# Spreading a block's scatters over the next block, and three smaller moves, in a macaron layer on one core

## The chip, the cores and the metric

One Trainium2 chip, one of its cores. The time is the device time in microseconds of one launch of the whole program; a few launches are timed and their median is given. Beside it stands one execution that the hardware profiler recorded; all durations below come from that one.

## The reference, cut to what matters

4096 tokens of width 256 (two sequences of 2048) go through three residual steps: half a feed-forward step, attention, half a feed-forward step again, each on a layer-normed input.

```python
x = x + 0.5 * ffn(layernorm(x))
x = x + attn(layernorm(x))
x = x + 0.5 * ffn(layernorm(x))
...
# ffn
logits = rmsnorm(x) @ router_w.T            # 8 experts, the best 2 of them for each token
dispatch = first 640 tokens of each expert  # in token order
routed   = scatter_add(w * (silu(xg @ rg) * (xg @ ru)) @ rd)   # inner width 1024
shared   = (silu(x @ sg) * (x @ su)) @ sd                      # inner width 2048
return shared + routed
...
# attn: groups of 64 tokens, 16 heads of 16
q, k = rmsnorm(q) * ln_w, rmsnorm(k) * ln_w
y = softmax(causal(q @ k.T / 4)) @ v
return y @ w_proj
```

The two feed-forward steps use the same weights. Float32 results are wanted; the kernel gets them from float16 matmuls by splitting each operand into a high and a low float16 part and summing three products.

## The kernel before

**Names of the work.** A *tile* is 128 tokens, a *block* is 512 tokens or four tiles; there are 32 tiles and 8 blocks. The shared expert's inner width of 2048 is cut into 16 *chunks* of 128. For a chunk and a block, `gate_up` (L339) runs 12 matmuls of 512 columns into two PSUM tiles `pgu` (three buffers; 6 for the gate, 6 for the up projection). ScalarE reads the gate's `pgu` into `sl` (L356 in phase c, L360 elsewhere), VectorE multiplies the gate's `pgu` into it (L357, phase c alone) and then the other `pgu` (L362), ScalarE rounds `sl` to the high part `hh` (L364), VectorE takes the low part `hl` (L365). `down` (L368) then adds 12 matmuls of 256 columns into two PSUM tiles `po`: 8 of them read `hh`, 4 read `hl`. `defer` emits the `down` of a chunk after the `gate_up` of the next one. After the 16th chunk, L406 evicts the two `po` tiles into `xr` on VectorE, and L409 stores them.

**Phases.** Phase a normalises and routes all 32 tiles for the first feed-forward step while it runs shared blocks 0 to 3. Phase b runs the 8 experts of that step. Phase c runs shared blocks 4 to 7 of the first step and blocks 0 to 6 of the second, and beside them attention on all 32 tiles, each followed by the norm and the routing for the second step. Phase d has the experts of the second step and the last shared block.

**What a tile does beside the blocks.** A tile's work is a generator whose steps are *slots*. `drive` (L728) takes one slot for every 3 steps of the shared block in phase c (`RATE_C`), so a block of 48 steps has 16 slots; a new tile starts every `GAP_C` = 4 slots. An attention tile: `stats` (L142) on VectorE and a power on GpSimd (L150, the reciprocal root), `normed` (L152) with a small VectorE instruction for the bias (`nm`, L158) and ScalarE for the result (L160), a DMA transpose, q, k, v matmuls, the squares of q and k on ScalarE (L544), their scaling on VectorE (L545) and a power on GpSimd (L547), q and k scaled on VectorE (L557) and spread on ScalarE (L567, L573) and GpSimd (L568, L574), scores, mask (L590), maximum (L595), exponential, values, projection, and then `stats` and `normed` again for the next step.

**Routing.** When the fourth tile of a block has its logits, `route` (L237) finds the two experts of each token and the row of the expert's list that it gets, and then scatters the tile rows `X` into the list `xg` in DRAM: for each of four tiles, four GpSimd copies (L328) of token number, weights and expert into the row's tail, and two indirect DMAs on GpSimd's queue (L330). One step of `route` issues one tile's scatters, so the four tiles go in four slots in a row. In phase c each is placed behind the last `anchor`, a GpSimd subtraction of an attention tile; phase a sets no anchor.

**Experts.** `expert_load` (L416) loads the 640 list tails of an expert (`tag`, L420) and the 640 rows, transposed (`xe`, L422), and turns the tails into row numbers and weights with four small VectorE instructions (L429 to L433). They are needed at the expert's last chunk, when its output is scattered.

**Order.** The program is emitted in the order above, and a scheduler then lays the instructions out on each engine; `issue_after` puts an instruction behind a given one on its engine, and `behind` does so for the last `gate_up` instructions on ScalarE (0) or VectorE (1). Each engine runs its own queue strictly in order; SyncE's queue issues the plain and transposing DMAs, GpSimd's the indirect ones.

Of the kernel before, what the change touches and what calls it, by code (L numbers as in the profile page):

```python
# [8 lines left out]
F32 = mybir.dt.float32  # L9
# [28 lines left out]
class Net:  # L38
# [103 lines left out]
    def stats(self, x, mv, rstd):  # L142
        nc = self.nc
        st = self.sm.tile([P, 6], F32, name="st")
        nc.vector.bn_stats(out=st, in_=x)
        nc.vector.bn_aggr(out=mv, in_=st)
        ve = self.sm.tile([P, 1], F32, name="ve")
        nc.vector.tensor_scalar(
            out=ve, in0=mv[:, 1:2], scalar1=LN_EPS, scalar2=1.0 / UP ** 2, op0=ALU.add, op1=ALU.mult)
        nc.gpsimd.tensor_tensor(out=rstd, in0=ve, in1=self.mhalf[:, :1], op=ALU.pow)  # L150

    def normed(self, x, mv, rstd, pool=False):  # L152
# [3 lines left out]
        if pool:  # L156
            nm = self.sm.tile([P, 1], F32, name="nm")
            nc.vector.scalar_tensor_tensor(  # L158
                out=nm, in0=mv[:, 0:1], scalar=-1.0, in1=rstd, op0=ALU.mult, op1=ALU.mult)
            nc.scalar.activation(z, x, AF.Identity, bias=nm, scale=rstd)  # L160
# [75 lines left out]

    def route(self, R, b, fb):  # L237

# [60 lines left out]
        if b == NB - 1:  # L299
            self.limits(R)  # L300
            yield
        for t in range(4):
            with self.tc.issue_after(self.anchor.ins) if self.anchor else nullcontext():
                self.scatter(R, b, fb, t, di, w1, dl, ef)
            yield

# [32 lines left out]
    def gate_up(self, wc, x, h, tanh=False):  # L339
# [24 lines left out]
        nc.scalar.copy(h[0], s)  # L364
        nc.vector.tensor_tensor(out=h[1], in0=s, in1=h[0], op=ALU.subtract)  # L365
        yield
# [25 lines left out]
    def shared(self, b, xb, src, dst, tanh=False, late=2):  # L392
        nc = self.nc
        outs = [self.ps_out.tile([P, BT], F32, name="po", tag="po") for _ in range(2)]
        for c in range(16):
# [5 lines left out]
            def fin(c=c, h=h):  # L401
# [3 lines left out]
                for i in range(2):  # L405
                    nc.vector.scalar_tensor_tensor(  # L406
                        out=res[i], in0=outs[i].rearrange("p (t f) -> p t f", f=H), scalar=0.5 / WS,
                        in1=res[i], op0=ALU.mult, op1=ALU.add)
                    nc.sync.dma_start(  # L409
# [6 lines left out]
    def expert_load(self, R, e, hold):  # L416
# [11 lines left out]
        tk = self.sm.tile([P, 5], I32, name="tkb")  # L428
        nc.vector.tensor_tensor(out=tk, in0=tag[:, :, 0].bitcast(I32), in1=R["bits"][:, e], op=ALU.bitwise_and)  # L429
        nc.vector.tensor_tensor(out=ids, in0=tk.bitcast(F32), in1=R["off"][:, e], op=ALU.add)  # L430
        nc.vector.scalar_tensor_tensor(
            out=w, in0=tag[:, :, 3], scalar=float(e), in1=tag[:, :, 1], op0=ALU.is_equal, op1=ALU.mult)
        nc.vector.tensor_tensor(out=w, in0=w, in1=tag[:, :, 2], op=ALU.add)  # L433

# [84 lines left out]
    def attn_tile(self, R, j, x2, new_fb):  # L519
# [23 lines left out]
        for i in range(2):  # L543
            nc.scalar.activation(qk[:, i, :], pqk[:, i, :], AF.Square, scale=1.0 / XP, accum_out=ss[:, i:i + 1])  # L544
        nc.vector.tensor_scalar(  # L545
            out=ss, in0=ss, scalar1=XP ** 2 / H, scalar2=1e-6 * XP ** 2, op0=ALU.mult, op1=ALU.add)
        nc.gpsimd.tensor_tensor(out=ss, in0=ss, in1=self.mhalf[:, :2], op=ALU.pow)  # L547
        pv = self.m1([P, H], F32, "pv")
# [136 lines left out]
class Tiles:  # L685


    def __init__(self, make, count, gap, held=None):
        self.make, self.count, self.gap = make, count, gap
        self.held = held  # L690
        self.slot = 0
        self.live = []
        self.nxt = 0

    def done(self):
        return self.nxt == self.count and not self.live

    def steps(self):

        if self.slot == self.nxt * self.gap and self.nxt < self.count:  # L700
            self.live.append((self.nxt, self.make(self.nxt)))
            self.nxt += 1
        for one in list(self.live):
# [4 lines left out]
            elif r == "stall":  # L708
                return
            yield  # L710
        self.slot += 1
# [36 lines left out]
def macaron(ctx, tc, x, w_qkv, ln_w, w_proj, router_w, rg, ru, rd, sg, su, sd, out):  # L748
# [21 lines left out]
    def tail(R, h, b, t):  # L770
        if t == 3:
            yield from n.route(R, b, fbs[(h, b)])

# [64 lines left out]
RATE_C = 3.0  # L838
GAP_C = 4
XTB = 2  # L840
# [31 lines left out]
```

## Time and profile before

| | us |
|---|---|
| median of 3 runs (lowest, highest) | 1819.73 (1818.86, 1820.77) |
| the profiled execution | 1819.79 |
| its span, first to last instruction | 1817.6 |
| TensorE busy | 1778.5 (98%) |
| VectorE busy | 1190.9 (66%) |
| ScalarE busy | 949.4 (52%) |
| GpSimd busy | 753.4 (41%) |
| scatters L330, 128 of them | 132.3 busy, 27.7 idle on "issue" in between |

The profiled execution lies within the spread of the timed runs, and 2.2 us lie outside its span. How to read it: TensorE is busy for nearly the whole span, so the sum of the other engines' work says little; what matters is where TensorE stands idle and which instruction ends that idle time. In a timeline row, the bracket gives the idle time of the engine just before the instruction and what ended it. A matmul's record is longer than the distance between two starts in a row (records overlap in the pipeline), so an idle bracket of TensorE is somewhat shorter than the time lost there.

### The profile page before, as it was taken

How to read it: one execution, taken by the hardware profiler on the slowest of the kernel's cores; microseconds unless marked ns; L12 is line 12 of the kernel's file. 1: busy time of each engine (PE TensorE's matmuls, PEld its weight loads, DVE VectorE, ACT ScalarE, POOL GpSimd, SP SyncE). 2: the span in 40 equal slices, each digit the busy share in tenths (PEclk: the TensorE clock that was granted, in tenths of full speed). 3: DMA queues.
4: the chain of work that ended last, by engine and by line, in shares of the span. 5: the costliest groups of instructions: out<-in, count | busy, mean ns of one | idle time of the engine just before them, and what ended most of it. 6: DMA issues, size and time to landing. Idle time of an engine off the chain costs nothing. (4 is left out here: it accounts for less than half of the span.)

```text
span 1817.6 us, 37398 instructions
## 1 busy us (share of the span) xinstructions
PE 1778.5 (98%) x13652; PEld 1199.6 (66%) x13652; DVE 1190.9 (66%) x2907; ACT 949.4 (52%) x2055; POOL 753.4 (41%) x1072
## 2 busy tenths in 40 slices
PE   8999999999999899999999999999999999999998
PEld 5665657777777556665656666566655677777765
DVE  7756546666665577877787777777756566666643
ACT  4433334555555466666666666666323455555542
POOL 6576620221111434576767677776430011122210
PEclk9999999999999999999999999999999999999999
DMA  7333133554443455767667676756212144555420
GB/s 216 91 102 112 41 66 84 123 118 111 114 108 71 98 91 101 129 112 141 122 134 135 117 152 111 145 98 127 61 28 66 35 108 109 116 121 118 103 44 12
DMA packets 439193, 185.95 MB, mean 102 GB/s; under 512 B 302305, under 2 KB 436125, under 8 KB 439008
## 3 DMA queue, kind: packets, MB, share of 16 engines
q1 hardware_dynamic: 420528, 161.60, 40.6%
q0 software_dynamic: 17664, 21.17, 6.7%
q8 instruction: 107, 1.75, 0.4%
q10 hardware_dynamic: 816, 0.79, 0.1%
q14 instruction: 78, 0.64, 0.1%
HBM read 78.95 MB, written 42.21 MB: 67 GB/s over the span
## 5 line engine op out<-in xcount | busy, mean ns | idle before, releaser
L349 PE MATMUL pgu<-xb,sgu 128*128 128x512 f16 x3072 | 736.6, 379 | 11.3 <-DVE sl L357 6.9
L364 ACT CAST hh<-sl 128x512 f16<-128x512 f32 (+2 forms) x512 | 272.9, 533 | 529.8 <-DVE sl L362 528.6
L349 PE MATMUL pgu<-xe,wc 128*128 128x384 f16 (+1 forms) x3072 | 497.1, 299 | 0.0
L349 PEld LDWEIGHTS <-sgu 128*128 128x128 f16 x3072 | 292.8, 98 | 284.7 <-issue 16.9
L362 DVE SCALAR_TENSOR_TENSOR sl<-pgu,sl 128x512 f32<-128x512 f32 (+2 forms) x512 | 301.0, 588 | 223.5 <-PE pgu L349 198.1
L365 DVE TENSOR_TENSOR hl<-sl,hh 128x512 f16<-128x512 f32 (+2 forms) x512 | 312.6, 611 | 149.3 <-ACT hh L364 147.9
L373 PEld LDWEIGHTS <-hh 128*128 128x128 f16 x3328 | 321.2, 98 | 109.8 <-ACT hh L364 6.6
L349 PEld LDWEIGHTS <-wc 128*128 128x128 f16 x3072 | 300.6, 98 | 92.0
L373 PE MATMUL po<-sdw,hh 128*128 128x256 f16 x2048 | 350.2, 273 | 5.3 <-ACT hh L364 3.2
L373 PE MATMUL po<-sdw,hl 128*128 128x256 f16 x1024 | 249.8, 273 | 14.0 <-DVE hl L365 11.4
L373 PE MATMUL po<-wd,hh 128*128 128x256 f16 x1280 | 223.6, 273 | 0.0
L472 POOL DMA_INDIRECT out_dram<-eo,eidscatter x40 | 65.2, 1630 | 341.3 <-DVE eo L471 331.6
L373 PEld LDWEIGHTS <-hl 128*128 128x128 f16 x1664 | 162.7, 98 | 56.3 <-DVE hl L365 22.6
L360 ACT ACTIVATE sl<-pgu 128x384 f32<-128x384 f32 (+1 forms) x336 | 159.0, 474 | 60.6 <-PE pgu L349 34.4
L472 POOL DMA_INDIRECT acc<-eo,eidscatter x40 | 65.7, 1642 | 290.3 <-DVE eo L471 280.6
L357 DVE SCALAR_TENSOR_TENSOR sl<-sl,pgu 128x512 f32<-128x512 f32 x176 | 120.2, 683 | 56.1 <-ACT sl L356 54.9
L330 POOL DMA_INDIRECT xg<-X,di x128 | 132.3, 1033 | 49.9 <-issue 27.7
L373 PE MATMUL po<-wd,hl 128*128 128x256 f16 x640 | 152.5, 273 | 0.0
L356 ACT ACTIVATE sl<-pgu 128x512 f32<-128x512 f32 x176 | 104.3, 593 | 39.1 <-PE pgu L349 37.5
L105 ACT ACTIVATE wc<-re 128x512 f16<-128x512 f32 x128 | 80.5, 629 | 74.4 <-PE pgu L349 58.2
L106 DVE SCALAR_TENSOR_TENSOR wc<-re,wc 128x512 f16<-128x512 f32 x128 | 88.3, 690 | 27.6 <-ACT wc L105 27.4
L596 POOL TENSOR_TENSOR S<-S,amx 128x1024 f32<-128x1024 f32 x32 | 63.9, 1997 | 77.9 <-DVE amx L595 70.9
(155 smaller groups left out, 1725.7 us busy)
## 6 DMA issues: line engine op xcount, KB each, us to landing
re<-in_L_ffn_rg_dram SPq DMA_DIRECT2D x128, 128.0 KB, 2.3
re<-in_L_ffn_ru_dram SPq DMA_DIRECT2D x128, 128.0 KB, 2.4
re<-in_L_ffn_rd_dram SPq DMA_DIRECT2D x128, 128.0 KB, 2.3
y<-acc SPq DMA_DIRECT2D x64, 128.0 KB, 2.4
y<-in_L_attn_x_dram SPq DMA_DIRECT2D x32, 128.0 KB, 2.2
acc<-xr SPq DMA_DIRECT2D x16, 256.0 KB, 2.5
out_dram<-xr SPq DMA_DIRECT2D x16, 256.0 KB, 2.7
x<-y SPq DMA_DIRECT2D x28, 128.0 KB, 1.9
```

Of the source, the lines that this page charges most:

```text
L105: nc.scalar.mul(hi, src, WS)
L106: nc.vector.scalar_tensor_tensor(out=lo, in0=src, scalar=WS, in1=hi, op0=ALU.mult, op1=ALU.subtract)
L330: i = nc.gpsimd.indirect_dma_start(out=R["xg"][:, :], out_offset=bass.IndirectOffsetOnAxis(ap=di[:, t, k:k + 1], axis=0), in_=X, in_offset ...
L349: nc.tensor.matmul(p, lhsT=wc[:, w, i, k, :], rhs=x[:, 2 * a + k, :], start=(j == 0), stop=(j == 5))
L356: nc.scalar.activation(s, p, AF.Tanh, scale=0.5 / XP)
L357: nc.vector.scalar_tensor_tensor(out=s, in0=s, scalar=1.0, in1=p, op0=ALU.add, op1=ALU.mult)
L360: self.latest[0] = nc.scalar.activation(s, p, AF.Silu, scale=1.0 / XP).ins
L362: self.latest[1] = nc.vector.scalar_tensor_tensor(out=s, in0=ps[1], scalar=1.0 / XP / (2.0 * XP if tanh else 1.0), in1=s, op0=ALU.mult, op ...
L364: nc.scalar.copy(h[0], s)
L365: nc.vector.tensor_tensor(out=h[1], in0=s, in1=h[0], op=ALU.subtract)
L373: nc.tensor.matmul(o, lhsT=h[a][:, t * P:(t + 1) * P], rhs=wd[:, w], start=(c == 0 and j == 0 and t % 2 == 0), stop=(c == nch - 1 and j == 2),
L472: i = nc.gpsimd.indirect_dma_start(out=R["acc"][:, :], out_offset=bass.IndirectOffsetOnAxis(ap=ids[:, t:t + 1], axis=0), in_=eo, in_offset ...
```

## The change

Four things are done, two of them by giving the scheduler further rules.

1. **Scatters.** `route` no longer runs its four scatter steps itself. They become a generator, `scatters`, handed to `Tiles.extra`; every slot, after the live tiles, takes one step of each such generator. One tile's scatters are issued every `int(gap)` slots: 4 in phase c, 2 in phase a. The last block of each step (`b == NB - 1`) keeps one tile per step. Each tile's scatters go behind the last `anchor`, and `stats` and the power on q's and k's squares now set the anchor too, so there is always one, in phase a as well.
2. **Distance of tiles.** `GAP_C` is 4.25 in place of 4, and a tile starts at the first slot that is not below its number times the gap: slots 0, 5, 9, 13, 17 and so on.
3. **Operands of powers.** GpSimd does the bias `nm` as a product and a multiplication by -1, and the scaling of the squares, in place of VectorE.
4. **Order on VectorE.** The second of the two evictions of a block is placed behind the low part of the chunk just emitted (`self.low`). The four small instructions of `expert_load` are placed behind the last `gate_up` instruction on VectorE.

```diff
 def stats(self, x, mv, rstd):
-        nc.gpsimd.tensor_tensor(out=rstd, in0=ve, in1=self.mhalf[:, :1], op=ALU.pow)
+        self.anchor = nc.gpsimd.tensor_tensor(out=rstd, in0=ve, in1=self.mhalf[:, :1], op=ALU.pow)
 def normed(self, x, mv, rstd, pool=False):
-            nc.vector.scalar_tensor_tensor(
-                out=nm, in0=mv[:, 0:1], scalar=-1.0, in1=rstd, op0=ALU.mult, op1=ALU.mult)
+            nc.gpsimd.tensor_tensor(out=nm, in0=mv[:, 0:1], in1=rstd, op=ALU.mult)
+            nc.gpsimd.tensor_scalar_mul(nm, nm, -1.0)
 def route(self, R, b, fb, tiles):
+        last = self.scatters(R, b, fb, di, w1, dl, ef, 1 if b == NB - 1 else tiles.gap)
+        if b == NB - 1:
+            yield from last
+        else:
+            tiles.extra.append(last)
+
+    def scatters(self, R, b, fb, di, w1, dl, ef, every):
         for t in range(4):
-            with self.tc.issue_after(self.anchor.ins) if self.anchor else nullcontext():
+            with self.tc.issue_after(self.anchor.ins):
                 self.scatter(R, b, fb, t, di, w1, dl, ef)
-            yield
+            for _ in range(int(every)):
+                yield
 def gate_up(self, wc, x, h, tanh=False):
-        nc.vector.tensor_tensor(out=h[1], in0=s, in1=h[0], op=ALU.subtract)
+        self.low = nc.vector.tensor_tensor(out=h[1], in0=s, in1=h[0], op=ALU.subtract).ins
 def shared(...):
                 for i in range(2):
-                    nc.vector.scalar_tensor_tensor(
+                    with self.tc.issue_after(self.low) if i else nullcontext():
+                        nc.vector.scalar_tensor_tensor(
 ...
 def expert_load(self, R, e, hold):
-        nc.vector.tensor_tensor(out=tk, in0=tag[:, :, 0].bitcast(I32), in1=R["bits"][:, e], op=ALU.bitwise_and)
+        with self.behind(True, 1):
+            nc.vector.tensor_tensor(out=tk, in0=tag[:, :, 0].bitcast(I32), in1=R["bits"][:, e], op=ALU.bitwise_and)
 ...
 def attn_tile(self, R, j, x2, new_fb):
-        nc.vector.tensor_scalar(
+        nc.gpsimd.tensor_scalar(
             out=ss, in0=ss, scalar1=XP ** 2 / H, scalar2=1e-6 * XP ** 2, op0=ALU.mult, op1=ALU.add)
-        nc.gpsimd.tensor_tensor(out=ss, in0=ss, in1=self.mhalf[:, :2], op=ALU.pow)
+        self.anchor = nc.gpsimd.tensor_tensor(out=ss, in0=ss, in1=self.mhalf[:, :2], op=ALU.pow)
 class Tiles:
-        if self.slot == self.nxt * self.gap and self.nxt < self.count:
+        if self.slot >= self.nxt * self.gap and self.nxt < self.count:
 ...
+        for g in list(self.extra):
+            if next(g, "end") == "end":
+                self.extra.remove(g)
+            yield
         self.slot += 1
-GAP_C = 4
+GAP_C = 4.25
```

More of the change, by code (lines that the diff above doesn't have):

```diff
@@ L235, in logits, with route @@
         nc.scalar.copy(fb["L"][:, t], p)
-    def route(self, R, b, fb):
+    def route(self, R, b, fb, tiles):
         nc = self.nc
@@ L405, in fin @@
                 for i in range(2):
-                    nc.vector.scalar_tensor_tensor(
-                        out=res[i], in0=outs[i].rearrange("p (t f) -> p t f", f=H), scalar=0.5 / WS,
-                        in1=res[i], op0=ALU.mult, op1=ALU.add)
+                    with self.tc.issue_after(self.low) if i else nullcontext():
+                        nc.vector.scalar_tensor_tensor(
+                            out=res[i], in0=outs[i].rearrange("p (t f) -> p t f", f=H), scalar=0.5 / WS,
+                            in1=res[i], op0=ALU.mult, op1=ALU.add)
                     nc.sync.dma_start(
@@ L428, in expert_load @@
         tk = self.sm.tile([P, 5], I32, name="tkb")
[L429 to L433, printed above, removed]
+        with self.behind(True, 1):
+            nc.vector.tensor_tensor(out=tk, in0=tag[:, :, 0].bitcast(I32), in1=R["bits"][:, e], op=ALU.bitwise_and)
+            nc.vector.tensor_tensor(out=ids, in0=tk.bitcast(F32), in1=R["off"][:, e], op=ALU.add)
+            nc.vector.scalar_tensor_tensor(
+                out=w, in0=tag[:, :, 3], scalar=float(e), in1=tag[:, :, 1], op0=ALU.is_equal, op1=ALU.mult)
+            nc.vector.tensor_tensor(out=w, in0=w, in1=tag[:, :, 2], op=ALU.add)
     def experts(self, R, rg, ru, rd, cur):
@@ L692, in __init__ @@
         self.live = []
+        self.extra = []
         self.nxt = 0
     def done(self):
-        return self.nxt == self.count and not self.live
+        return self.nxt == self.count and not self.live and not self.extra
     def steps(self):
-        if self.slot == self.nxt * self.gap and self.nxt < self.count:
+        if self.slot >= self.nxt * self.gap and self.nxt < self.count:
             self.live.append((self.nxt, self.make(self.nxt)))
@@ L771, in tail @@
         if t == 3:
-            yield from n.route(R, b, fbs[(h, b)])
+            yield from n.route(R, b, fbs[(h, b)], tiles)
     def tile1(j):
```

## The prediction

> **What bounds the kernel now.** I read the page's first part, then busy time by stretch, then looked for every idle bracket of TensorE in the timeline, and last at who holds the instruction that ends it.
>
> ```profile
> PE 1778.5 (98%) x13652; PEld 1199.6 (66%) x13652; DVE 1190.9 (66%) x2907; ACT 949.4 (52%) x2055; POOL 753.4 (41%) x1072
> ```
>
> TensorE is busy for all but 39.1 of 1817.6 us, and the change takes no matmul away. So the most that any reordering can give is these 39 us, about 2%. By stretch (columns: stretch, length, then busy PE, PEld, DVE, ACT, POOL, granted clock, DMA share, GB/s):
>
> ```profile
> 0.00:266.00 266.00, 255.37 (x1698) 154.96 (x1699) 162.49 (x527) 105.11 (x222) 154.60 (x345) 0.99 0.39 107
> 594.00:660.00 66.00, 59.70 (x367) 34.04 (x366) 41.64 (x83) 36.23 (x79) 26.77 (x33) 1.00 0.46 89
> 660.00:1300.00 640.00, 626.22 (x5296) 396.56 (x5295) 492.23 (x1240) 405.27 (x851) 429.48 (x580) 1.00 0.65 121
> 1300.00:1381.00 81.00, 77.40 (x483) 45.51 (x482) 48.79 (x133) 25.66 (x48) 18.23 (x40) 1.00 0.27 59
> ```
>
> Idle: 10.6 us in phase a, 6.3 at the entry of phase c, 13.8 in its steady part, 3.6 at its end; 4.2 are the end of the program. Both expert stretches between have none. In phase a, one place:
>
> ```profile
> 136.33 0.98 POOL L330 DMA_INDIRECT xg<-X,di  x1 [0.30 <-issue]
> 137.45 0.59 POOL L150 TENSOR_TENSOR rstd<-ve,mhalf 128x1 f32<-128x1 f32 x1
> 138.07 0.41 DVE L162 TENSOR_SCALAR z<-y,mv,rstd 128x256 f32<-128x256 f32 x1 [5.08 <-POOL rstd L150]
> 138.49 0.66 DVE L365 TENSOR_TENSOR hl<-sl,hh 128x512 f16<-128x512 f32 x1
> 139.21 0.28 PE L373 MATMUL po<-sdw,hl 128*128 128x256 f16 x1 [2.27 <-DVE ve L148]
> ```
>
> Read upward: TensorE waits for the low part, which stands on VectorE behind L162, which waits for a power on GpSimd, which stands behind eight scatters of 1.28 us each (0.98 and 0.30 of issue). In phase c the same wait for `hl` comes back in every block, with other culprits:
>
> ```profile
> 909.26 0.59 ACT L356 ACTIVATE sl<-pgu 128x512 f32<-128x512 f32 x1
> 909.88 0.69 DVE L357 SCALAR_TENSOR_TENSOR sl<-sl,pgu 128x512 f32<-128x512 f32 x1 [0.55 <-ACT sl L356]
> 910.62 1.46 PE L349 MATMUL pgu<-xb,sgu 128*128 128x512 f16 x6 [0.87 <-DVE sl L357]
> 911.28 0.68 DVE L406 SCALAR_TENSOR_TENSOR xr<-po,xr 128x512 f32<-128x512 f32 x1
> 912.48 0.68 DVE L406 SCALAR_TENSOR_TENSOR xr<-po,xr 128x512 f32<-128x512 f32 x1
> 913.08 0.68 DVE L365 TENSOR_TENSOR hl<-sl,hh 128x512 f16<-128x512 f32 x1
> 913.82 0.28 PE L373 MATMUL po<-sdw,hl 128*128 128x256 f16 x1 [0.71 <-DVE hl L365]
> 934.31 0.28 PE L373 MATMUL po<-sdw,hl 128*128 128x256 f16 x1 [0.74 <-DVE hl L365]
> ```
>
> These three waits (a `pgu` buffer freed late, `hl` behind both evictions and a mask, and 20 us later `hl` behind mask and maximum, L590 and L595) recur every 81.5 us, because 4 slots per tile and 16 per block keep tiles and blocks in step. At the end of phase c small expert instructions, waiting for their DMAs, hold VectorE:
>
> ```profile
> 1378.69 0.17 DVE L429 TENSOR_TENSOR tkb<-tag,scatter1b 128x5 int32<-128x5 int32 x1 [0.60 <-DMA tag<-xg]
> 1379.60 0.68 DVE L406 SCALAR_TENSOR_TENSOR xr<-po,xr 128x512 f32<-128x512 f32 x1
> 1380.34 0.38 PE L373 MATMUL po<-sdw,hh 128*128 128x256 f16 x2 [2.01 <-DVE xr L406]
> ```
>
> **The change part by part.** A bracket is about 0.16 us short of the time lost, since records overlap; I add that to each. Where places are counted I use the order in which the built program puts instructions on each engine, which has no times in it.
>
> *Scatters.* Their number, 128, their four copies each and their DMAs stay. A burst of 8, 10.3 us, becomes four of 2.6 us, each behind a power. Phase a has three stalls at such bursts: 42.86 (1.75 us), 139.21 (2.43), 168.18 (0.54). The one at 139 costs more:
>
> ```profile
> 139.60:143.10 3.50, 3.50 (x14) 1.59 (x12) 3.03 (x19) 1.52 (x3) 0.93 (x5) 0.51 0.51 138
> ```
>
> After 2.27 idle us the granted clock was 0.51 for 3.5 us, so another 1.7 us of matmul time went. The Trainium skill (TensorE: Matmul & The Clock Gate, Part 1) has the clock fall only after at least one idle window of some 3.4 us; by that rule the stall is worth 2.4 us, by the row 4.1. I take the row. With half of the other two (a power may still wait 2.6 us), phase a gives 5.2 of 6.4. What could it cost? Rows `X` stay occupied longer: tile 4 of a block scatters some 19 slots after its norm, its buffer (one of 6) is wanted after 25.5; 6 slots of 5 us are left, so nothing.
>
> *Evictions.* At six boundaries 0.87 us is lost, 5.2 in all. In the new order the first eviction still precedes `hl` at times, the second never, so `hl` comes at least 0.6 us sooner; one boundary has the key and value instructions L552, L557 in front of `hl` instead, and I leave it its loss: 4.4. The added wait: behind the second eviction on VectorE stands the next L357, and on SyncE a store; on TensorE the second half of the new block's `down`, before which the order has 6 gate/up matmuls (1.29 us) against 0.68 of eviction. Zero.
>
> *4.25 slots.* Tiles now drift by one slot per block. I summed, for each chunk of phase c, VectorE's work between L362 and its L365 and set it against the matmul work placed before the first use of `hl`. Before, the stalled chunks are those with 1.9 to 2.0 us in between and 5.1 to 5.3 us of cover, a difference of 3.1 or 3.4; no other chunk in the steady part is below 3.7. In the new order chunks with so much work have 6 us of cover or more, differences of 4.0 and up; two chunks stay below 3.4. So the five stalls of 0.90 behind mask and maximum leave 3.6 of 4.5. The six `pgu` waits of 1.04 (6.2 us) come from ScalarE, where L356 stands behind L567; that happens in three tiles of four now, in one of four then: I take half, 3.1. The last tile starts at slot 132, not 124. In the new order the last routing matmul (L311) stands 33 us of matmul work later but still 48 us ahead of the first expert matmul; from the first of the last scatters (1344.99) to the first split of expert weights (1362.74) the trace has 17.8 us. Nothing is due there.
>
> *Expert instructions.* Moved from the phase's end to some chunk of each expert, with one DMA of tails per expert moved on SyncE past weight loads (their two buffers allow it one expert ahead, some 38 us). The stalls of 1364 to 1380 sum to 4.6. ScalarE's first split stands 12 us behind L311 in the new order against 17.8 needed from nearly there, so part stays: 3.0 gained. Inside experts TensorE has no idle time though more VectorE work (scaling L471 and splits) lies there; four instructions of 0.16 cost zero. If that cover were gone it would be 14 times 0.5 us.
>
> *GpSimd forms operands.* VectorE loses 64 x 0.159 and 32 x 0.169 = 15.6 us and these waits (us in total, times, longest):
>
> ```profile
> DVE nm L158 <- POOL rstd L150: 23.3, 15, 2.8
> DVE nm L158 <- POOL arstd L150: 8.3, 20, 0.7
> ```
>
> GpSimd gains 64 products and 64 scalings; the nearest rows are L244 (0.21) and L245 (0.24 to 0.37), so 0.44 to 0.58 a pair, and 0.24 to 0.37 for the squares: 36 to 49 us over phase c, where it goes from 67% to about 73%. The Trainium skill (GPSIMD Engine Reference, Engine selection) speaks against this: element-wise work belongs on VectorE, GpSimd being about twice as slow on two inputs. The row agrees on the price (0.44 against 0.16), and by the rule alone the sum would be 64 x 0.28 = 18 us of longer chains. But the trace puts the wait between the engines (31.6 us of VectorE standing) above the arithmetic, and these chains have slots to spare. Own value: zero (from -16 as below to +2).
>
> *New waits.* In the new order five places of phase c have ScalarE work between two L356 that exceeds the matmul work by over 1.3 us, against three before. I charge them and a tighter entry of phase c 4.1 us.
>
> Sum: 5.2 + 4.4 + 3.6 + 3.1 + 3.0 - 4.1 = 15.2 us; 1819.79 - 15.2 = 1804.6. The profiled execution is within 0.1 us of the median, so this is also the median that I expect.
>
> **The rivals.** *The stalls move* (0.20). The waits depend on lateness that an order without times doesn't show; half of the 19.3 us goes, the new waits come: 1819.8 - 9.6 + 4.1 = 1814.3. For it: before, three equal stalls per block survived a planned order. Against: the differences of work and cover pick out the stalled chunks.
>
> *GpSimd's longer chain makes it slower* (0.13). The power for q and k now stands behind two subtractions (0.67 each) close in front of it in 14 tiles of 32 and one in 12 (before: 3 and 11), and has one more instruction. If ScalarE's L567, waiting for it, has L356 behind it, `pgu` is freed up to 1.4 us later. With all 15.2 us gained, it decides from 11 tiles on; at 18 tiles, 25 us, the time is 1830. Against: in three tiles of four L356 stands ahead of L567.
>
> *It does not do what it says* (0.07): the spread scatters hold the powers as before, or the late last tile delays the experts, and gains are returned: 1819, slightly slower possible.
>
> **How the numbers follow.** Forecast 0.60, at 1804.6. A measurement of this kernel tells about 0.2% (3.6 us) from no change. Faster: 0.60 and 0.17 of the first rival, 0.77. Same: 0.03 of it and 0.05 of the last, 0.08. Slower: 0.13 and 0.02, 0.15. The range leaves out the slow rival (0.13) above 1819, and below 1796 the case that nearly all of 29 us of stalls goes (0.07).
>
> **What would show it.** Right: no idle bracket over 2 us at the scatters of phase a and no half clock there; no L158 or L545 among VectorE's rows; idle of 660 to 1300 down from 13.8 to 5 or 6; no wait for `tag` on VectorE near the end of phase c. Wrong: brackets of 1 us for L349 behind L357 in most blocks, with L567 waiting for L547's successor on GpSimd; or a new wait for `hl` once per block.

## The result: slower by 0.9%, and the profile after

The changed kernel takes 1834.61 us (median of 6 runs, 1833.94 to 1836.77) against 1819.7 us of the kernel before beside it; the ratio is 1.0087, with a 95% interval of 1.0077 to 1.0097. That is 30 us above the forecast of 1804.6 and outside its range. The profiled execution has a span of 1832.4 us against 1817.6.

The first line is the busy time of the changed kernel's page. In it `gate_up`'s VectorE instructions are L366 and L371, the high part is L373, the low part L374, `down` is L382.

```profile
PE 1781.5 (97%) x13652; PEld 1198.9 (65%) x13652; DVE 1202.6 (66%) x2811; ACT 949.5 (52%) x2055; POOL 802.5 (44%) x1232
```

VectorE has 96 instructions fewer, which were 15.6 us in the profile before, and is busy 11.7 us longer. That is the first sign that something else got slower. Then busy time by stretch (length, busy PE, PEld, DVE, ACT, POOL, granted clock, DMA share, GB/s):

```profile
0.00:257.00 257.00, 251.49 (x1697) 154.10 (x1698) 163.46 (x525) 106.24 (x222) 154.17 (x345) 0.99 0.40 111
585.00:651.00 66.00, 59.02 (x350) 32.87 (x349) 37.08 (x71) 33.07 (x68) 28.11 (x43) 0.97 0.37 77
651.00:1315.00 664.00, 634.25 (x5237) 395.79 (x5236) 500.05 (x1131) 403.12 (x851) 455.10 (x689) 1.00 0.64 116
1315.00:1396.00 81.00, 79.72 (x575) 49.23 (x573) 56.11 (x124) 30.15 (x55) 34.51 (x75) 1.00 0.24 52
1396.00:1448.50 52.50, 49.92 (x309) 30.01 (x308) 28.25 (x49) 16.55 (x29) 6.66 (x7) 1.00 0.29 62
```

TensorE stands idle 5.5 us in phase a, 7.0 at the entry of phase c, 29.8 in its steady part (13.8 before) and 3.9 at its end: 1.3 up to 1396 and 2.6 from there to the experts (3.6 and none in the kernel before). So phase a went as forecast or better, the entry is 0.7 us and the end 0.3 us worse, and the steady part of phase c, from which some 8 us of idle time were to go, has 16 us more. (The stretches are cut by time and hold somewhat different work: 5237 matmuls in the steady part in place of 5296.) Cut by the experts' gate and up matmuls, which give clean borders:

| us of the profiled execution | phase a | phase b | phase c | phase d |
|---|---|---|---|---|
| before | 274.2 | 314.0 | 845.4 | 384.0 |
| after | 265.2 | 314.0 | 869.3 | 383.9 |

Phase a gained 9.0 us, phase c lost 23.9. What follows is about phase c. These are TensorE's longest waits over the whole program (us in total, times, longest), before and after:

```profile
PE po L373 <- DVE hl L365: 11.4, 16, 1.6
PE pgu L349 <- DVE sl L357: 6.9, 9, 0.9
PE po L373 <- ACT hh L364: 3.2, 7, 1.1
```

```profile
PE po L382 <- ACT hh L373: 11.3, 18, 1.7
PE pgu L358 <- DVE sl L366: 10.7, 14, 1.6
PE po L382 <- DVE hl L374: 5.9, 9, 1.2
PE pl L228 <- DMA xb<-X: 4.1, 5, 1.6
```

The waits for `hl`, at which much of the change was aimed, did fall by half. What grew are the waits for `hh` and `sl`, which stand in the queues of ScalarE and VectorE, and for the transposed rows `xb` (0.3 us before). Two things stand out in the rows. One is a wait that passes through ScalarE:

```profile
965.19 2.13 POOL L618 TENSOR_TENSOR e<-S,e 128x1024 f16<-128x1024 f32 x1
967.28 0.40 POOL L159 TENSOR_SCALAR nm<-nm 128x1 f32<-128x1 f32 x2
967.55 0.60 ACT L160 ACTIVATE z<-y,nm,rstd 128x256 f32<-128x256 f32 x1 [2.74 <-POOL nm L159]
969.86 0.62 ACT L373 CAST hh<-sl 128x512 f16<-128x512 f32 x1
970.53 0.61 PE L382 MATMUL po<-sdw,hh 128*128 128x256 f16 x4 [0.83 <-ACT hh L373]
...
979.57 1.90 POOL L607 TENSOR_TENSOR S<-S,amx 128x1024 f32<-128x1024 f32 x1 [4.99 <-DVE amx L606]
980.77 1.24 DVE L374 TENSOR_TENSOR hl<-sl,hh 128x512 f16<-128x512 f32 x1 [0.57 <-ACT hh L373]
```

The scheduler put the 2.1-us subtraction for `e` between the two GpSimd instructions that now form the bias `nm`, so ScalarE waits 2.74 us for it, `hh` stands behind `z` in ScalarE's queue, and TensorE behind `hh`. The last two rows show the second thing: a low part that usually takes 0.69 us takes 1.24 while GpSimd subtracts. Over the whole program (a tile's groups: count, then least, median and longest ns of one; first before, then after):

```profile
L365 DVE TENSOR_TENSOR hl<-sl,hh x512: 411/607/2203, 19.0 to 1811.3; 128x512 f16<-128x512 f32 x86, 128x256 f16<-128x256 f32 x43, 128x384 f16<-128x384 f32 x42
```

```profile
L374 DVE TENSOR_TENSOR hl<-sl,hh x512: 409/606/2549, 17.9 to 1826.1; 128x512 f16<-128x512 f32 x86, 128x256 f16<-128x256 f32 x43, 128x384 f16<-128x384 f32 x42
```

The median is the same; the tail is not. Adding up what each `hl` took above the median of its shape, where it is more than 0.1 us, gives 11.0 us (19 instructions) before and 22.5 us (36) after. This sum is called *the stretch of hl* below.

### The profile page after: what moved, and what is told of

Read it like the earlier page. It is cut to its first block, busy times and chain, and to the rows that moved or that the text cites. A ratio compares the mean times of both kernels' runs of the same rounds, so it can differ in the third digit from the quotient of the medians.

```text
span 1832.4 us, 37477 instructions
## 1 busy us (share of the span) xinstructions
PE 1781.5 (97%) x13652; PEld 1198.9 (65%) x13652; DVE 1202.6 (66%) x2811; ACT 949.5 (52%) x2055; POOL 802.5 (44%) x1232
## 4 chain that ended last, share of the span: by engine, by line
PE 50%; issue 16%; DVE 10%; POOL 10%; DMA 6%; ACT 6%; SPq 2%; DVEq 0%; POOLq 0%; ACTq 0%
PE pgu L358 32%; PE po L382 16%; DMA QT<-QK 2%; DVE sl L371 2%; DVE sl L366 1%; DMA acc<-eo,eidscatter 1%; DVE hl L374 1%; POOL S L607 1%; ACT hh L373 1%; POOL xg L339 1%; ACT V L611 1%; DVE S L601 1%; DVE amx L606 1%; POOL acc L483 1%; SPq L432 1%
## 5 line engine op out<-in xcount | busy, mean ns | idle before, releaser
L373 ACT CAST hh<-sl 128x512 f16<-128x512 f32 (+2 forms) x512 | 272.9, 533 | 505.9 <-DVE sl L371 502.7
L374 DVE TENSOR_TENSOR hl<-sl,hh 128x512 f16<-128x512 f32 (+2 forms) x512 | 324.0, 633 | 209.4 <-ACT hh L373 208.1
L371 DVE SCALAR_TENSOR_TENSOR sl<-pgu,sl 128x512 f32<-128x512 f32 (+2 forms) x512 | 301.1, 588 | 238.0 <-PE pgu L358 204.0
L382 PEld LDWEIGHTS <-hh 128*128 128x128 f16 x3328 | 320.8, 98 | 125.3 <-ACT hh L373 20.8
L382 PE MATMUL po<-sdw,hh 128*128 128x256 f16 x2048 | 350.3, 273 | 13.6 <-ACT hh L373 11.3
L382 PE MATMUL po<-sdw,hl 128*128 128x256 f16 x1024 | 250.2, 273 | 7.2 <-DVE hl L374 5.9
L382 PE MATMUL po<-wd,hh 128*128 128x256 f16 x1280 | 223.6, 273 | 0.0
L382 PEld LDWEIGHTS <-hl 128*128 128x128 f16 x1664 | 162.7, 98 | 49.6 <-DVE hl L374 14.0
L339 POOL DMA_INDIRECT xg<-X,di x128 | 136.2, 1064 | 47.4 <-issue 22.0
L382 PE MATMUL po<-wd,hl 128*128 128x256 f16 x640 | 152.5, 273 | 0.0
L366 DVE SCALAR_TENSOR_TENSOR sl<-sl,pgu 128x512 f32<-128x512 f32 x176 | 119.7, 680 | 39.2 <-ACT sl L365 37.6
L365 ACT ACTIVATE sl<-pgu 128x512 f32<-128x512 f32 x176 | 104.1, 591 | 49.1 <-PE pgu L358 41.0
L106 DVE SCALAR_TENSOR_TENSOR wc<-re,wc 128x512 f16<-128x512 f32 x128 | 88.3, 690 | 25.6 <-ACT wc L105 25.4
```

The costliest lines, as they stand in the source:

```text
L106: nc.vector.scalar_tensor_tensor(out=lo, in0=src, scalar=WS, in1=hi, op0=ALU.mult, op1=ALU.subtract)
L339: i = nc.gpsimd.indirect_dma_start(out=R["xg"][:, :], out_offset=bass.IndirectOffsetOnAxis(ap=di[:, t, k:k + 1], axis=0), in_=X, in_offset ...
L365: nc.scalar.activation(s, p, AF.Tanh, scale=0.5 / XP)
L366: nc.vector.scalar_tensor_tensor(out=s, in0=s, scalar=1.0, in1=p, op0=ALU.add, op1=ALU.mult)
L371: self.latest[1] = nc.vector.scalar_tensor_tensor(out=s, in0=ps[1], scalar=1.0 / XP / (2.0 * XP if tanh else 1.0), in1=s, op0=ALU.mult, op ...
L374: self.low = nc.vector.tensor_tensor(out=h[1], in0=s, in1=h[0], op=ALU.subtract).ins
```

## Experiments

Each kernel ran beside runs of the kernel before on the same chip, whose median lay between 1818.8 and 1826.0 us from one group of runs to the next; so ratios to it are compared, not times. "Phase c" is the length as in the table above, 845.4 us before. Line numbers shift by a few from kernel to kernel; the names of the tiles tell the instruction. One reserve holds for nearly all that follows: the scheduler plans phase c anew for each kernel, so a comparison of two kernels compares two orders as well. In the traces, `a_scat` has the order of the kernel before on every engine in phase c and `only_evict` departs from it in eight places on VectorE and one on TensorE; the others have clearly different orders.

### Which part costs it? Two parts taken out, two done alone

`u_ops` is the changed kernel with the powers' operands back on VectorE:

```diff
-            nc.gpsimd.tensor_tensor(out=nm, in0=mv[:, 0:1], in1=rstd, op=ALU.mult)
-            nc.gpsimd.tensor_scalar_mul(nm, nm, -1.0)
+            nc.vector.scalar_tensor_tensor(
+                out=nm, in0=mv[:, 0:1], scalar=-1.0, in1=rstd, op0=ALU.mult, op1=ALU.mult)
...
-        nc.gpsimd.tensor_scalar(
+        nc.vector.tensor_scalar(
             out=ss, in0=ss, ...)
```

> The changed kernel with the bias and the scaling of the squares back on VectorE; scatters, 4.25 slots and both orders on VectorE stay. Theory A (GpSimd's longer chain holds ScalarE's norm, and hh behind it, in phase c): the 24 us that phase c lost go, 1811. Theory B (4.25 slots puts tiles where the planned order does not hold on the chip): the loss stays, 1828 to 1835. Theory C (spread scatters hold GpSimd's other work in phase c): stays, 1828 to 1835.

Measured: 1817.76 us, ratio 0.9966 (0.9954 to 0.9977). Phase c is 852.6 us.

`u_gap` is the changed kernel with tiles 4 slots apart:

```diff
-GAP_C = 4.25
+GAP_C = 4
```

> The changed kernel with 4 slots between tiles; all else stays. Theory A: 1828 to 1835, ScalarE still waits some 30 to 40 us for nm. Theory B: the steady blocks of phase c fall back to about 81.5 us or less, 1811. Theory C: 1828 to 1835.

Measured: 1818.52 us, ratio 0.9968 (0.9956 to 0.9981). Phase c is 852.9 us.

`only_scat` is the kernel before with the spread scatters and their new anchors alone:

```diff
+        last = self.scatters(R, b, fb, di, w1, dl, ef, 1 if b == NB - 1 else tiles.gap)
...
-        nc.gpsimd.tensor_tensor(out=rstd, in0=ve, in1=self.mhalf[:, :1], op=ALU.pow)
+        self.anchor = nc.gpsimd.tensor_tensor(out=rstd, in0=ve, in1=self.mhalf[:, :1], op=ALU.pow)
```

> The kernel before with the spread scatters and their anchors alone. Theories A and B: phase a gains its 9 us and phase c is as before, 1811. Theory C: phase a gains 9 us and phase c loses 15 to 24, 1826 to 1835.

Measured: 1829.16 us, ratio 1.0029 (1.0017 to 1.0040). Phase a is 266.2 us (8.0 less than before), phase c 863.5 (18.1 more).

`only_ops` is the kernel before with the operands on GpSimd alone (the first diff the other way round).

> The kernel before with bias and scaling of the squares on GpSimd alone. Theory A: 1835 to 1843 (the 15 to 24 us of phase c without the 9 of phase a). Theories B and C: 1820, within 3.

Measured: 1836.96 us, ratio 1.0071 (1.0054 to 1.0088). Phase c is 861.6 us.

Each of the three theories got its own part right and failed on the others. Taking either the operands or the 4.25 slots out of the change gives back 1.2 points and leaves a kernel 0.3% faster than before; yet the operands alone cost 0.7%, and the scatters alone, the part that gains in phase a, cost 0.3%. Such sums do not tell the parts apart; they depend on each other. The rows of `only_scat` show one thing that they share. These come once in each of five blocks (GpSimd, VectorE and TensorE at one place):

```profile
963.36 1.08 POOL L339 DMA_INDIRECT xg<-X,di  x1 [0.19 <-POOL ss L558]
964.75 0.97 POOL L339 DMA_INDIRECT xg<-X,di  x1 [0.30 <-issue]
965.75 0.68 POOL L170 TENSOR_TENSOR X<-z,X 128x256 f16<-128x256 f32 x1
966.38 0.67 POOL L170 TENSOR_TENSOR xa<-z,xa 128x256 f16<-128x256 f32 x1
967.01 1.28 POOL L579 TENSOR_TENSOR QK<-qk,QK 128x256 f16<-128x256 f32 x2
968.26 1.15 POOL L585 TENSOR_TENSOR QK<-qk,QK 128x512 f16<-128x512 f32 x1
968.41 3.41 DVE L374 TENSOR_TENSOR hl<-sl,hh 128x512 f16<-128x512 f32 x1
969.38 1.89 POOL L607 TENSOR_TENSOR S<-S,amx 128x1024 f32<-128x1024 f32 x1
971.88 0.40 PE L382 MATMUL po<-sdw,hl 128*128 128x256 f16 x1 [2.77 <-DVE hl L374]
```

Two scatters stand in front of GpSimd's subtractions, which then run without a pause up to 971.27. `hl`, started at 968.41 in the middle of them, ends at 971.82, 0.55 us after the last, so nearly all of its 0.69 us of work comes when GpSimd is through. In the kernel before, GpSimd has a gap at the answering place, between the subtraction for `QK` and that for `S`:

```profile
910.57 1.17 POOL L574 TENSOR_TENSOR QK<-qk,QK 128x512 f16<-128x512 f32 x1
915.03 1.90 POOL L596 TENSOR_TENSOR S<-S,amx 128x1024 f32<-128x1024 f32 x1 [3.30 <-DVE amx L595]
```

In `only_scat` TensorE waits 2.77 us for `hl`, and then shows a granted clock of 0.60 (window, columns as above):

```profile
972.10:975.50 3.40, 3.40 (x16) 1.95 (x15) 2.87 (x9) 1.28 (x3) 0.65 (x1) 0.60 1.00 142
```

In `only_ops` the same happens beside another group of GpSimd instructions: an `hl` of 0.69 us takes 3.05 beside a power and the subtraction for `e`, which ends at 998.82. There `hl` gets its turn, up to 999.38, and now the product for `nm` takes 0.65 us in place of 0.19:

```profile
996.18 0.56 POOL L150 TENSOR_TENSOR arstd<-ve,mhalf 128x1 f32<-128x1 f32 x1
996.33 3.05 DVE L370 TENSOR_TENSOR hl<-sl,hh 128x512 f16<-128x512 f32 x1 [0.68 <-ACT hh L369]
996.70 2.12 POOL L614 TENSOR_TENSOR e<-S,e 128x1024 f16<-128x1024 f32 x1
998.78 0.65 POOL L158 TENSOR_TENSOR nm<-mv,rstd 128x1 f32<-128x1 f32 x1
999.44 0.28 PE L378 MATMUL po<-sdw,hl 128*128 128x256 f16 x1 [1.67 <-DVE hl L370]
```

The stretch of `hl` is 11.0 us before, 22.5 in the changed kernel, 16.6 in `u_ops`, 15.1 in `u_gap`, 30.1 in `only_scat`, 34.4 in `only_ops`. The Trainium skill has a rule for it (SBUF — State Buffer, sections SBUF: two separate sides and Who interferes with whom): VectorE and GpSimd share one pair of ports; a VectorE instruction with two inputs in SBUF contends with a GpSimd instruction that reads SBUF, whoever starts first has the pair for its whole instruction, and the other fully blocks. This blocking is called *the hold* below. `hl = sl - hh` has two SBUF inputs.

### The theory of the hold: `hl` read from PSUM

If that is the cause, an `hl` with one input in PSUM is not held. In phase c, `sl` is therefore left in the PSUM bank from which its second factor comes, and both parts are taken from there:

```diff
-            out=s, in0=ps[1], scalar=..., in1=s, op0=ALU.mult, op1=ALU.mult).ins
-        nc.scalar.copy(h[0], s)
-        nc.vector.tensor_tensor(out=h[1], in0=s, in1=h[0], op=ALU.subtract)
+            out=ps[1] if tanh else s, in0=ps[1], scalar=..., in1=s, op0=ALU.mult, op1=ALU.mult).ins
+        nc.scalar.copy(h[0], ps[1] if tanh else s)
+        nc.vector.tensor_tensor(out=h[1], in0=ps[1] if tanh else s, in1=h[0], op=ALU.subtract)
```

(`tanh` is true in phase c alone.) GpSimd's instructions stay. It is done to the kernel before as a control, to the changed kernel, and to the two parts alone. The order of phase c changes with this edit too.

> The kernel before, with one thing else in the phase of the second attention layer (176 chunks of the shared expert): sl is left in its PSUM bank and the high part hh and the low part hl are taken from there, so that hl = sl - hh has one SBUF input and one PSUM input and not two SBUF inputs. The planner re-plans the order a little for it. This is the control for three others. Theory L (hl, with two SBUF inputs, is held by GpSimd's subtractions; in the trace of before hl is stretched by 11.0 us over its median in all, in the changed kernel by 22.5): hl rows over 1 us in that phase vanish, and about 0.7 of 11.0 us lies on the path: 1808 to 1817 us against 1819.7. Theory Q (the loss of the changed kernel is the order in ScalarE's and GpSimd's queues, the stretch is only seen): 1817 to 1823. Theory P (the price: the bank is held until hl is read, some 1.3 us longer, and gate and up matmuls wait for it): above 1825, with more waits of TensorE's gate and up matmuls for VectorE.

Measured: 1810.23 us, ratio 0.9952 (0.9935 to 0.9968). Phase c is 837.4 us, 8.0 less.

> The changed kernel with the same: in the second attention layer's phase hh and hl are taken from the PSUM bank. Theory L: 0.7 of the 22.5 us by which hl is stretched goes, so 1812 to 1822 against 1834.6, and it gains more than the kernel before does by the same edit. Theory Q: 1828 to 1838, hl short but hh as late as before. Theory P: above 1836.

Measured: 1809.31 us, ratio 0.9945 (0.9928 to 0.9961). Phase c is 843.8 us, 25.5 less than in the changed kernel.

> The kernel before with the scatters spread one tile at a time (as in only_scat, 1829.2 us), and with hh and hl taken from the PSUM bank in the second attention layer's phase. In only_scat one hl of each of five blocks took 3.4 us, each was followed by 3.4 us at half clock, and hl was stretched by 30.1 us in all. Theory L: 0.7 of 30.1 and about 8 us of half clock go: 1798 to 1812, the fastest so far. Theory Q (two scatters of 1 us each stand ahead of the K subtraction in GpSimd's queue, so K, S and the scores come late whatever hl does): 1822 to 1830. Theory P: above 1830.

Measured: 1802.78 us, ratio 0.9916 (0.9899 to 0.9933). Phase c is 837.9 us, 25.6 less than in `only_scat`.

> The kernel before with the powers' operands formed on GpSimd (as in only_ops, 1837.0 us), and with hh and hl taken from the PSUM bank in the second attention layer's phase. In only_ops hl was stretched by 34.4 us in all, one of each of six blocks to 3.0 us, while GpSimd went through a power, the subtraction for e (2.1 us) and the product for nm without a pause. Theory L: 0.7 of 34.4 goes: 1808 to 1820. Theory Q (z waits on ScalarE for nm, which stands behind a 2.1-us subtraction, and hh waits behind z): 1830 to 1840. Theory P: above 1838.

Measured: 1827.94 us, ratio 1.0048 (1.0031 to 1.0064). Phase c is 855.1 us, 6.5 less than in `only_ops`.

Two of the four fall inside the range of the theory of the hold, the changed kernel 2.7 us below it, and `pl_ops` well above. The rows are as the theory has them in all four; this is `hl` in `pl_scat`, outside and inside phase c:

```profile
L374 DVE TENSOR_TENSOR hl<-sl,hh x336: 415/558/737, 18.2 to 1794.2; 128x384 f16<-128x384 f32 x128, 128x512 f16<-128x512 f32 x40
L374 DVE TENSOR_TENSOR hl<-pgu,hh x176: 651/691/693, 590.7 to 1418.4; 128x512 f16<-128x512 f32 x176
```

No `hl` of phase c is above 0.694 us in any of the four. Because the order changed too, the cleanest reading is inside one trace. Of the phase's low parts, take those that overlap one of GpSimd's two-input subtractions by more than 0.1 us and those that do not:

| mean us of an `hl` in phase c | overlapping | not overlapping |
|---|---|---|
| changed kernel, both inputs in SBUF | 1.045 (64) | 0.690 (109) |
| the same with `hl` from PSUM | 0.687 (83) | 0.686 (93) |
| `only_scat` | 1.195 (60) | 0.686 (114) |
| `pl_scat` | 0.688 (71) | 0.686 (105) |

Overlap costs 0.36 to 0.51 us on the average where both inputs are in SBUF, and nothing where one is in PSUM. The skill's rule holds here.

It holds the other way round as well. In phase c of the changed kernel 84 of GpSimd's instructions (scatters aside) took over 0.1 us more than the median of their kind, 34.5 us together. Every one of them overlaps an `hl`, and in 83 cases the `hl` had started first. The kernel before has 44 such instructions with 14.2 us, and in the kernels with `hl` from PSUM none overlaps an `hl`. As an example, the subtraction that makes `xa` (least, median, longest ns), in the changed kernel and in `pl_after`:

```profile
L170 POOL TENSOR_TENSOR xa<-z,xa x32: 660/672/1184, 608.8 to 1278.2; 128x256 f16<-128x256 f32 x32
L170 POOL TENSOR_TENSOR xa<-z,xa x32: 662/672/687, 610.1 to 1247.9; 128x256 f16<-128x256 f32 x32
```

So the change added 11.5 us of held `hl` and 20.3 us of held GpSimd work. The second kind does not show as a wait for `hl`; it can reach TensorE through ScalarE, which waits for GpSimd's results (`z` for `nm`, `S` for its subtraction) with `hh` behind it.

With the hold gone, the changed kernel and the kernel before are equal (0.9945 and 0.9952), and 17.5 of the 23.9 us of phase c are gone. How much of the 17.5 is the hold and how much the new order is not shown: the changed kernel gains 25.5 us by the edit, more than the 22.5 by which `hl` was stretched. For the hold speaks that phase c is shorter in all seven pairs of kernels that differ in this edit (the four here and three below), by 6.5 to 25.6 us, each with another order.

The miss is `pl_ops`: the hold is gone there, and it still takes 17.7 us more in phase c than `pl_before`. The other theory, ScalarE's queue, expected 1830 to 1840 and is nearer. Its wait is in the trace, smaller but still there (ScalarE's wait for `nm`: us in total, times, longest), first in `only_ops`, then in `pl_ops`:

```profile
ACT z L160 <- POOL nm L159: 65.3, 28, 4.0
```

```profile
ACT z L160 <- POOL nm L159: 38.8, 28, 3.0
```

Some 12 us of the 17.7 stand in the phase's first three blocks. There TensorE waits 2.9 us for the transposes of q and k, 2.9 for `xb` and 2.1 for the transposed exponentials, against 1.3, none and 0.7 in `pl_before`; which instruction sets these waits off stays open.

### The other parts alone, and what they bring without the hold

`only_gap` is the kernel before with `GAP_C = 4.25` alone.

> The kernel before with the attention tiles 4.25 slots apart in the second phase, and nothing else of the change. The sum of the prediction (the mask and maximum of a tile and the gate and up matmuls' waits move off the repeated place): 3.6 and 3.1 us less, 1813. Theory L (a new order decides by which hl falls beside which subtraction on GpSimd; and 4.25 slots make the entry of the phase some 5 us longer and leave more attention work to its last block, as the changed kernel with 4 slots showed): 1820 to 1830, with hl stretched by more than 11 us.

Measured: 1863.91 us, ratio 1.0250 (1.0233 to 1.0267), phase c 890.4 us: far beyond both. The hold is a part (stretch of `hl` 24.4 us); the rows show another:

```profile
932.99 4.60 SPq L586 DMA_TRANSPOSE QT<-QK  x2
940.96 0.71 ACT L574 CAST QK<-qk 128x256 f16<-128x256 f32 x2 [4.13 <-DMA QT<-QK]
942.09 0.61 ACT L369 CAST hh<-sl 128x512 f16<-128x512 f32 x1
942.74 1.66 DVE L370 TENSOR_TENSOR hl<-sl,hh 128x512 f16<-128x512 f32 x1 [4.39 <-ACT hh L369]
942.76 0.39 PE L378 MATMUL po<-sdw,hh 128*128 128x256 f16 x2 [2.30 <-ACT hh L369]
944.45 0.40 PE L378 MATMUL po<-sdw,hl 128*128 128x256 f16 x1 [1.30 <-DVE hl L370]
```

ScalarE may not write a `QK` buffer before the transposing DMA has read what it held. Here the two transposes of one tile were issued from 932.99 to 937.59, behind another transpose on SyncE's queue, and the next tile's copy, whose turn on ScalarE came at 936.8, waited 4.13 us; `hh` behind it made TensorE wait 2.30, and then the held `hl` 1.30 more. Over the program this wait went from the first line (before) to the second (`only_gap`):

```profile
ACT QK L567 <- DMA QT<-QK: 2.2, 1, 2.2
```

```profile
ACT QK L574 <- DMA QT<-QK: 27.1, 6, 5.9
```

`only_evict` is the kernel before with the second eviction behind the low part alone:

```diff
+                    with self.tc.issue_after(self.low) if i else nullcontext():
```

> The kernel before with the second eviction of a block issued behind the next low part, and nothing else. The sum of the prediction: the stall of 0.9 us at each block's start goes at the places where it was seen, 4.4 us less: 1815.3. Rival: the PSUM bank of the output is freed 0.7 us later and the stall moves to the first down matmul: 1818 to 1822.

Measured: 1818.82 us, ratio 1.0000 (0.9991 to 1.0008): no change. The rows answer to those at 910.62, 913.82 and 934.31 of the kernel before, 1.2 us later:

```profile
911.79 1.46 PE L354 MATMUL pgu<-xb,sgu 128*128 128x512 f16 x6 [0.87 <-DVE sl L362]
914.38 0.28 PE L378 MATMUL po<-sdw,hl 128*128 128x256 f16 x1
...
935.46 0.28 PE L378 MATMUL po<-sdw,hl 128*128 128x256 f16 x1 [0.88 <-DVE hl L370]
```

The bracket of 0.71 at `hl` is gone, as forecast. But some of it comes back at the matmuls just behind, 20 us later `hl` is waited for 0.88 us in place of 0.74, and the scores in between have a new wait of 0.14. Counted by the distance between the starts of matmuls, TensorE loses 3.1 us in this block before and after, and the block is 81.5 us long as before.

`pl_u_ops` is the changed kernel with operands on VectorE and `hl` from PSUM; `pl_u_ops_gap` has 4 slots besides.

> The changed kernel with the powers' operands back on VectorE and with hh and hl taken from the PSUM bank in the second attention layer's phase (so scatters spread, 4.25 slots, eviction, tag, and no hold on hl). Theory S (once hl is not held, the parts add up: operands on GpSimd cost 17.7 us, as between the kernel before with hl from PSUM, 1810.2, and the same with the operands on GpSimd, 1827.9): 1809.3 - 17.7 = 1792, 1788 to 1797. Theory N (they don't add up; what the operands cost at 4 slots is a place in ScalarE's queue that 4.25 slots move): 1799 to 1810.

Measured: 1809.12 us, ratio 0.9942 (0.9926 to 0.9959), phase c 845.5 us.

> The same with 4 slots: the kernel before with hl from PSUM, scatters spread, eviction and tag. Against the one without eviction and tag (1802.8). Theory S (they bring what the prediction's sum gave them, 4.4 and 3.0): 1795, 1792 to 1799. Theory N: 1800 to 1806. Beside the kernel with 4.25 slots of this call it tells what 4.25 slots are worth where hl is not held: S by the prediction's 6.7 us a loss here, N the other way round by the 3 to 6 us of the phase's entry and last block.

Measured: 1801.16 us, ratio 0.9908 (0.9891 to 0.9924), phase c 836.6 us. It is faster than both kernels.

Without the hold the operands on GpSimd cost nothing in the full change (0.9945 with, 0.9942 without), eviction and tag (the four expert instructions that read it) bring 0.08 points (0.9916 to 0.9908, which the intervals don't separate), and 4.25 slots cost 0.34 points. So theory N of these expectations held, and parts still don't add: at 4 slots and without the spread scatters, the operands cost 0.96 points.

### What the parts do where phase c keeps its order, or loses the hold

`a_scat` spreads the scatters in phase a and leaves phase c the burst and its old order (`tiles.gap` is 2 in phase a and 4 in phase c; the new anchors are set in phase a alone, not shown here):

```diff
-        last = self.scatters(R, b, fb, di, w1, dl, ef, 1 if b == NB - 1 else tiles.gap)
-        if b == NB - 1:
+        last = self.scatters(R, b, fb, di, w1, dl, ef, 1 if b == NB - 1 or tiles.gap > 2 else tiles.gap)
+        if b == NB - 1 or tiles.gap > 2:
```

> The kernel before with the scatters spread one tile at a time in the first phase only; in the second attention layer's phase the scatters stay in one run, as before, and the order of TensorE's instructions there is that of before. Theory L: the 9 us that the first phase gained in the changed kernel come whole, and nothing is lost later: 1808 to 1813. Rival (what the first phase gains is waited for later, as the experts' phase starts with other loads under way): 1815 to 1821.

Measured: 1815.30 us beside 1826.01 of the kernel before; ratio 0.9943 (0.9927 to 0.9960), about 10 us. In its trace phase a is 267.9 us and phase c 847.4; `pl_gap`, run beside it with the burst in phase a, has a phase a of 275.5. Over all traces phase a is 273.5 to 275.6 us in the seven kernels with the burst and 264.5 to 267.9 in the ten with spread scatters, 8.2 us less on the average. So some 8 of the 10 us are phase a's, and they are kept if phase c keeps its order; where the rest lies is open.

`pl_gap` is `only_gap` with `hl` from PSUM.

> The kernel before with 4.25 slots alone (as in only_gap, 1863.9 us), and with hh and hl taken from the PSUM bank in the second attention layer's phase. In only_gap hl was stretched by 24.4 us in all, and eight spells at half clock followed stalls that hh and hl made together. Theory L: both go, 1810 to 1830. Theory Q (hh is late in ScalarE's queue behind QK's and V's copies, and the run of scatters on GpSimd stands behind it, whatever hl does): 1840 to 1866.

Measured: 1843.60 us beside 1826.01; ratio 1.0097 (1.0080 to 1.0114). By the ratio this is between the two theories: of the 2.5% of `only_gap`, 1.5 points go. Against `pl_before` (0.9952) 4.25 slots still cost 1.45 points here, and the wait that has nothing to do with `hl` is still there:

```profile
ACT QK L574 <- DMA QT<-QK: 22.9, 6, 5.7
```

`u_ops_gap` is the changed kernel with operands on VectorE and 4 slots: spread scatters, eviction and tag remain, with `hl` in SBUF.

> The changed kernel with the powers' operands back on VectorE and with 4 slots: spread scatters, eviction and tag remain. The prediction's sum: 5.2 + 4.4 + 3.0 less, 1807. Theory L (the order of the second attention layer's phase is that of the spread scatters alone, where one hl of each block took 3.4 us): 1822 to 1830, with those rows again.

Measured: 1826.50 us beside 1826.01; ratio 0.9997 (0.9988 to 1.0005). The five low parts of 3.4 us are there again; the stretch of `hl` is 30.1 us, phase c 862.2. The three parts that the prediction gave 12.6 us bring nothing together, and against `only_scat` (1.0029) eviction and tag bring 0.32 points.

## Why the prediction was wrong, point by point

**The step that failed.** The prediction took its own value for the operands on GpSimd as zero, since "these chains have slots to spare", counted 6.7 us of gain for the 4.25 slots, and charged all new waits in phase c with 4.1 us. What it aimed at came in part: TensorE's idle time in phase c behind `hl` fell from 9.9 to 5.9 us. But its idle time there behind everything else rose from 13.7 to 33.3 us, some 20 us of new waits in place of 4.1.

**The cause that was missing.** The prediction priced every instruction at its median row and looked for waits between queues. The price of GpSimd's arithmetic was not the fault. GpSimd is busy 49.1 us longer where 36 to 49 were forecast, but that agreement is in part luck: with `hl` from PSUM in both kernels it is 31.8 us longer (762.8 against 731.0), and much of the rest is hold. What was missing is that work put on GpSimd, or moved on it, is also work beside which a two-input VectorE instruction stands still, and which stands still beside it. The profile before had the sign in its group of `hl`, the instruction that TensorE waited for most: median 607 ns, longest 2203. The chains were not free either: at 4 slots, with the hold gone, the operands still cost 17.7 us of phase c (`pl_ops` against `pl_before`). The slow rival had the right direction (1830) and a part of the mechanism. It looked to ScalarE's queue, and TensorE's waits that pass through it did grow: behind `hh` by 8.1 us, behind L366 by 3.8. In the row shown, though, ScalarE waits for the split `nm`, not for the power of q and k.

**The size of it.** Phase c lost 23.9 us. With `hl` from PSUM the changed kernel's phase c is 6.4 us longer than that of the control, so 17.5 us go with the edit. What the 6.4 are is not shown; the 4.25 slots alone cost 8.9 in the pair `pl_u_ops`, `pl_u_ops_gap`.

**Scatters in phase a: mechanism right, size low.** 5.2 us were taken, 9.0 came in the profile and 8.2 on the average of all traces. The three stalls at the scatters and the half clock behind one of them are gone whole, the 6.4 us of which a part had been left standing. What failed is the silence about phase c: the step said what a spread scatter may cost buffers, and not that two scatters of 1 us each then stand ahead of GpSimd's subtractions and close the gap between them (phase c is 18.1 us longer in `only_scat`).

**Evictions: 4.4 forecast, nothing came.** The order argument was right for the row that it was made for, and the time was lost again up to 20 us on. This is the first rival, "the stalls move", in its pure form.

**4.25 slots: 3.6 and 3.1 forecast as gains, a loss came.** It was the term furthest off: +2.5% alone, and 1.2 points inside the change. The difference of work and cover on VectorE per chunk was the wrong test: it does not see ScalarE held by a transposing DMA, nor instructions that are stretched. The late last tile, which was to cost nothing, had a price. The first load of an expert's list starts at 1405.6 in place of 1356.4 and waits 9.9 us for the last scatters; the experts' weights, loaded behind it, are split at 1412 to 1421, just ahead of the experts, and TensorE waits 2.6 us behind these splits.

**Expert instructions: 3.0 forecast.** The waits of VectorE for `tag` near the end of phase c are gone (6.4 us before), but the end has as much idle time as before, 3.9 us for 3.6, since the waits behind the splits have come. Eviction and tag together bring 0.08 to 0.32 points (1.5 to 5.8 us) in the two pairs that show them, and eviction alone nothing; so the term is of the right sign, and its size is not settled.

**The signs named beforehand.** No bracket above 2 us in phase a's scatters, no L158 on VectorE and no wait for `tag` there: right, and they say nothing about the end time. Idle of the steady part 5 or 6 us: wrong, 29.8. Brackets of about 1 us behind L366, a sign of failure, come at five places of the steady part (0.97 to 1.6 us), about as many as before (six of 0.87). "A new wait for `hl` once per block", the other such sign, is what `only_scat` shows, but not the changed kernel.

## What to carry to other kernels

Where VectorE's instruction with two SBUF inputs lies on the path to TensorE, GpSimd's work is not free even if its queue has room: look at the longest and not the median of that group, at what GpSimd runs beside it, and at GpSimd's own longest. Reading one input from PSUM where it already lies took the hold away, and phase c became shorter in each of the seven kernels tried; the kernel before gained 0.5% and the changed one 1.4 points. A new order of a tight pipeline should be taken apart on the chip before its parts are summed: here one part cost 0.7% or nothing, depending on the others.

## What the runs showed of the hardware that was not expected

A two-input VectorE subtraction on SBUF (0.69 us) took up to 3.42 us beside GpSimd instructions that followed each other without a gap. In the rows of `only_scat` it did not get in between two subtractions, nor between the power and the subtraction for `e` in those of `only_ops`; there it did get in before the next product, and that product was held in turn. With one input in PSUM it never went above 0.693 us in the changed kernel, at 83 overlaps, and GpSimd was not held by it either.

The granted clock fell after no more than 2.3 us of idle time, in two pieces. In the changed kernel two stalls of 0.63 and 1.65 us lie within 3.7 us, and the window behind the second shows a mean granted clock of 0.57:

```profile
622.55 1.46 PE L358 MATMUL pgu<-xb,sgu 128*128 128x512 f16 x6 [0.63 <-DVE sl L371]
625.65 0.61 PE L382 MATMUL po<-sdw,hh 128*128 128x256 f16 x4 [1.65 <-ACT hh L373]
```

```profile
626.00:629.50 3.50, 3.38 (x15) 1.71 (x13) 2.99 (x5) 1.61 (x3) 0.85 (x1) 0.57 1.00 143
```

Counting matmuls of 256 or more columns that start at twice the usual distance, such spells cost about 2 us before and in the changed kernel, 9 in `only_scat` and 12 in `only_gap`. The stall of 2.77 us shown from `only_scat` so costs another 1.4 us (estimate: 3.4 us at 0.60).
